# A gather-and-sum graph layer on one core: parts of x taken from its bytes, and the counts dealt to the turns from a table

## The chip, the cores and the metric

The kernel runs on one core of one Trainium2 chip. The metric is the time of one execution on the device, in microseconds. Three runs of the kernel before are given, and one further execution was profiled; all times of single instructions come from that one.

## The reference

One layer of a graph network with two kinds of edges, then a residual sum and a layer norm. There are 12500 nodes of 128 features, and 400000 edges, sorted by `dst`.

```python
Xs = X[src]
m_data = Xs @ W_data.T + b_data
m_ctrl = Xs @ W_control.T + b_control
msg = jnp.where((edge_types == 0)[:, None], m_data, m_ctrl)
agg = jax.ops.segment_sum(msg, dst, num_segments=X.shape[0])
out = jax.nn.relu(agg + (X @ W_self.T + b_self))
x = _layernorm(X + out, axis=-1)          # over the features, eps 1e-5, no scale, no shift
```

## The kernel before

**What it sums.** The weights are applied after the sums. For every node and each kind of edge the kernel sums the rows `x[src]` of its edges, and counts the edges (for the biases). Since the edges are sorted by `dst`, a stretch of edges touches few nodes, and a sum is a matrix product of rows with a 0/1 selection: rows on the partitions, two kinds times 88 nodes (176 columns) as the moving side.

**Exact rows from bf16.** A float32 row would be slow in the matrix engine, so x is split into three bf16 parts that add up to it, 384 columns instead of 128. They lie in SBUF (`x3`, 98 blocks of 128 nodes) and in DRAM (`rows3`). In `split_x` x is fetched in 8 pieces (six of 14 blocks, one of 13, and the last, partial block), four ahead of use, by DMAs on ScalarE's queue. Of each piece (`split`) ScalarE copies x to bf16 (the high part, line 262), VectorE subtracts that from x (line 263), ScalarE copies the rest to bf16 (the middle part, line 264), and VectorE subtracts again (the low part, line 265). The pieces are then stored to `rows3` on SP's queue.

**Two ways to the rows.** The 3125 chunks of 128 edges fall into 25 groups of 125 chunks, each with five runs of 5 chunks ("p") and five of 20 ("e"); in 18 of the groups the last e run is taken as p instead. A p chunk fetches its 128 rows from `rows3` by an indirect DMA on GpSimd's queue (line 754, tile `msg`). The 107 e windows `w` need no such fetch: their 2560 edges are sorted by the source's block of 128 nodes into 100 cells of 32 places (`block_matrix` to `keep_codes`: products on VectorE, small matrix products, a round trip through DRAM with the tiles `there` and `pick`), and the rows are picked out of `x3` by matrix products with a 0/1 matrix of 128 nodes by 32 places (line 820, `got<-x,pick`). Four blocks share a product's 128 output partitions, each in its own quarter of 32 columns of the array. Edges that find their cell full are fetched by an indirect DMA as well (line 798, tile `last`, one for each window).

**A window's turns.** In `picked`, the 25 fours of blocks of a window go in five turns, bounds 0, 5, 10, 15, 19, 24. Turn `t` picks the rows of its fours into PSUM (`rows`), ScalarE copies them to bf16 (line 834, tile `emsg`), VectorE makes selections (`choose`, line 504: 10 fours in turn 0, 9 in turn 1, 6 in turn 3, from two buffers), and TensorE adds the rows of the turn before to the window's sums (`add`, line 704, full width). The turn of 3 also picks the last, half four (quarters 2 and 3). Before `add`, `count` (line 842) adds up the edges of each four: a product of 32 columns, `one_col`, with the selection, put into quarter `q % 4`:

```python
cells_of(s["ps"], EW, 1)[CAP * (q % 4):CAP * (q % 4 + 1), :], one_col[:, :CAP], s["sel"][q],
```

The turns 1 to 4 count 5, 5, 5 and 4 fours; the end of the window, which is run within turn 0 of the next one, counts 6. The quarters are added up when a group is finished, so it does not matter which of them a four is counted in. `accumulate` then adds the window's sums to the group's (line 743).

**Order.** Units of work are merged by a position within the window (`merged`, `evenly`), and a scheduler of the framework sets the order of instructions on each engine from there; `issue_after` holds work behind a given instruction. `paced` lets a gather start behind a given matrix product.

**The opening.** Before the first window the kernel makes its tables, splits x (one unit a piece, `split_units`), prepares the e edges of group 0 (`prep_e`), sorts windows 0 and 1 (`all_slots`), computes where each window's sums go (`places_and_weights`), and stores `rows3`. Then the loop over the windows starts. A second, slow path for inputs on which the sorting overflows (`long_path`) is skipped at the end by a branch.

## Time and profile before

| what | us |
|---|---|
| median of 3 runs | 1758.43 |
| lowest and highest run | 1756.07, 1759.98 |
| the profiled execution | 1757.87 |
| its span, first to last instruction | 1756.1 |
| TensorE busy (matrix products) | 1615.3 |
| VectorE busy | 1595.2 |
| GpSimd busy | 1316.6 |
| ScalarE busy | 1229.2 |

PE is TensorE, PEld its weight loads, DVE VectorE, ACT ScalarE, POOL GpSimd, and SP the engine that issues most DMAs. A row of a group gives line, engine, operation, output and inputs with their shapes, the count, then the busy time and the mean of one in ns, then the idle time ahead of these instructions and who ended it. A row of the timeline gives the start, the duration, the engine and the same names, with the idle time in brackets; neighbouring instructions of one line are merged, and the duration runs to the end of the last. Matrix products overlap in the pipeline, so the distance from one start to the next tells more than a duration. A name with a q behind the engine is its queue: it waits or issues.

### The profile page before, as it was taken

What the parts mean: (1) busy time and instruction counts of PE and PEld (TensorE: products, weight loads), DVE (VectorE), ACT (ScalarE), POOL (GpSimd) and SP (SyncE); (2) the same over time, 40 slices, a digit from 0 to 9 for tenths busy, and PEclk for the clock granted to TensorE, in tenths of its full rate; (3) what the DMA queues carried; (4) which work ended last, traced back from release to release, by engine and by line L of the source; (5) the groups of instructions that cost most, each with busy time, mean ns of one, the idle gap of its engine ahead of it and who ended that gap; (6) DMA issues with size and microseconds to landing.
All of it is one profiled execution on the core that took longest, in us unless ns stands there. A gap on an engine that the chain in (4) does not pass through costs nothing.

```text
span 1756.1 us, 72083 instructions
## 1 busy us (share of the span) xinstructions
PE 1615.3 (92%) x29945; PEld 1311.7 (75%) x29945; DVE 1595.2 (91%) x3996; ACT 1229.2 (70%) x2249; POOL 1316.6 (75%) x1109
## 2 busy tenths in 40 slices
PE   0599999999999999999999999999999989999997
PEld 0377777777778777777877877777777777878786
DVE  8899999998999998999988999999999989999993
ACT  4577777767677667767766777776777766767675
POOL 0288877787777787877887877887877877777871
PEclk9999999999999999999999999999999999999999
DMA  8655454446454545444535454544454535544441
GB/s 237 209 165 160 128 158 136 147 125 199 115 164 134 159 125 179 143 152 127 166 119 164 150 164 133 164 122 147 160 159 135 158 108 162 167 139 141 151 139 41
DMA packets 190562, 261.28 MB, mean 149 GB/s; under 512 B 86437, under 2 KB 155983, under 8 KB 187152
## 3 DMA queue, kind: packets, MB, share of 16 engines
q1 hardware_dynamic: 126894, 148.02, 25.9%
q0 software_dynamic: 50704, 102.16, 20.8%
q10 hardware_dynamic: 12626, 6.40, 1.2%
q8 instruction: 236, 3.87, 0.9%
q14 instruction: 102, 0.84, 0.1%
HBM read 238.47 MB, written 18.00 MB: 146 GB/s over the span
## 4 chain that ended last, share of the span: by engine, by line
PE 48%; DVE 32%; issue 6%; DMA 6%; ACT 5%; DVEq 1%; POOL 1%; SPq 0%; POOLq 0%; ACTq 0%
PE sums L704 22%; PE got L820 15%; DVE esel L504 3%; PE side L950 3%; DVE pick L690 3%; PE sums L842 3%; DMA last<-rows,idx 3%; DVE rv L635 2%; ACT emsg L834 2%; DVE prod L598 2%; DVE prod L576 2%; PE side L584 2%; DVE acc L743 2%; PE side L647 2%; DVE ahead L594 2%
## 5 line engine op out<-in xcount | busy, mean ns | idle before, releaser
L754 POOL DMA_INDIRECT msg<-rows,pidx x985 | 1190.9, 1209 | 307.5 <-issue 118.9
L834 ACT CAST emsg<-got 128x768 bf16<-128x768 f32 (+1 forms) x1070 | 951.9, 930 | 303.9 <-PE got L820 289.8
L704 PE MATMUL sums<-esel,emsg 128*128 128x176 bf16 x7704 | 683.4, 240 | 0.0
L704 PEld LDWEIGHTS <-emsg 128*128 128x128 bf16 x7704 | 566.9, 98 | 68.7 <-issue 28.5
L820 PE MATMUL got<-x,pick 128*32 128x384 bf16 x10486 | 568.0, 330 | 21.9 <-DVE pick L690 14.7
L820 PEld LDWEIGHTS <-pick 128*32 128x32 bf16 x10486 | 239.2, 96 | 139.2 <-issue 20.6
L504 DVE TENSOR_TENSOR esel<-code_col,code 128x1760 bf16<-128x1760 bf16 x321 | 292.7, 912 | 13.6 <-PE sums L704 11.6
L798 POOL DMA_INDIRECT last<-rows,idx x107 | 122.0, 1141 | 106.0 <-DVE pick L690 63.7
L704 PE MATMUL sums<-psel,msg 128*128 128x48 bf16 x2955 | 184.2, 184 | 17.2 <-DVE acc L743 15.2
L842 PE MATMUL sums<-esel,one_col 128*32 128x176 bf16 x2675 | 193.7, 240 | 4.4 <-DVE acc L743 4.4
L704 PEld LDWEIGHTS <-msg 128*128 128x128 bf16 x2955 | 149.9, 97 | 36.2 <-issue 31.4
L842 PEld LDWEIGHTS <-one_col 128*32 128x32 bf16 x2675 | 111.9, 97 | 60.7 <-issue 4.1
L790 PE MATMUL sums<-psel,one_col 128*128 128x48 bf16 x985 | 150.2, 183 | 0.0
L743 DVE TENSOR_TENSOR acc<-acc,sums 128x352 f32 (+2 forms) x232 | 99.4, 430 | 40.4 <-PE sums L704 36.8
L504 DVE TENSOR_TENSOR O<-cell_col,blk 128x2000 bf16<-128x2000 bf16 x107 | 128.2, 1198 | 2.1 <-issue 2.1
L598 DVE TENSOR_TENSOR prod<-O,ahead 128x2000 bf16<-128x2000 bf16 x107 | 127.6, 1193 | 0.1
L690 DVE TENSOR_SCALAR pick<-pick,lane_f 128x3200 bf16<-128x3200 bf16 x107 | 113.2, 1058 | 0.0
L647 PE MATMUL side<-rv,O 128*128 128x64 bf16 x2140 | 83.3, 195 | 31.6 <-DVE rv L635 30.6
L647 PEld LDWEIGHTS <-O 128*128 128x128 bf16 x2140 | 78.7, 100 | 33.3 <-DVE rv L635 29.3
L594 DVE TENSOR_REDUCE ahead<-side 128x100 bf16<-128x500 f32 x107 | 72.2, 675 | 28.0 <-PE side L520 27.3
L790 PEld LDWEIGHTS <-one_col 128*128 128x128 bf16 x985 | 94.3, 96 | 0.0
L635 DVE TENSOR_TENSOR rv<-rm,vals 128x1280 bf16<-128x1280 bf16 x107 | 87.8, 821 | 0.3
(170 smaller groups left out, 1869.2 us busy)
## 6 DMA issues: line engine op xcount, KB each, us to landing
pick<-there SPq DMA_DIRECT2D x107, 800.0 KB
acc<-acc_start SPq DMA_DIRECT2D x23, 1280.0 KB
msg<-rows,pidx POOLq DMA_INDIRECT x985
rows<-x SPq DMA_DIRECT2D x6, 1344.0 KB
xs<-in_x_dram SPq DMA_DIRECT2D x99, 62.5 KB
out_dram<-h SPq DMA_DIRECT2D x99, 62.5 KB
xt<-in_x_dram ACTq DMA_DIRECT2D x6, 896.0 KB
there<-cell SPq DMA_DIRECT2D x107, 6.2 KB
```

Of the source, the lines that this page charges most:

```text
L504: nc.vector.tensor_tensor(sel.rearrange("p n (w t) -> p n w t", t=2), col[:rows].rearrange("p (o w t) -> p o w t", o=1, t=2).to_broadcast( ...
L598: nc.vector.tensor_tensor(prod, s["O"], ahead.rearrange("p (o j) -> p o j", o=1).to_broadcast([P, EC, NCELL]), op=OP.mult)
L635: placed[:] = [nc.vector.tensor_tensor(rv.rearrange("p c v (r t) -> p c v r t", t=2), rm.rearrange("p c (o r t) -> p c o r t", o=1, t=2).t ...
L647: nc.tensor.matmul(s["rk"][:m, :2 * CAP], s["held"][:, c * NCELL:c * NCELL + m], s["rv"][:, c].rearrange("p v r -> p (v r)"), start=(c == ...
L690: nc.vector.tensor_scalar(t, t, lane_f, None, op0=OP.is_equal)
L704: last = nc.tensor.matmul(out, msg[:, j * D:(j + 1) * D], sel, start=(start and j == 0), stop=stop, skip_group_check=True)
L743: added.append(nc.vector.tensor_add(win, win, ps[:, :4 * wide].rearrange("p (a w) -> p a w", w=wide)[:, :, :width]))
L754: return nc.gpsimd.indirect_dma_start(out=msg, out_offset=None, in_=rows3[:, :], in_offset=bass.IndirectOffsetOnAxis(ap=codes["p", g][0][: ...
L790: nc.tensor.matmul(cnt, one_col, sel, start=False, stop=(c == n - 1), skip_group_check=True)
L820: last = nc.tensor.matmul(ps[CAP * a:CAP * (a + 1), :], slots[w]["pick"][:, a * NQ + q, :], x3[:, 4 * q + a - a0].rearrange("p j d -> p (j ...
L834: nc.scalar.copy(msg[:, :n], ps[:, :n, :3 * D])
L842: nc.tensor.matmul(cells_of(s["ps"], EW, 1)[CAP * (q % 4):CAP * (q % 4 + 1), :], one_col[:, :CAP], s["sel"][q], start=(q < 4), stop=(q + 4 ...
```

## The change

The two parts below the high one are now made from the bytes of the float itself. ScalarE copies the upper 16 bits of each float to the high part; it also copies the second and the first byte, as numbers scaled by 2^-15 and 2^-23, to the middle and the low part. VectorE takes sign and exponent of the high part by an AND on 16-bit integers (tile `power`, a power of two) and multiplies both lower parts by it, in place.

The counts are dealt from a table, `quarters`: 4, 4, 8 and 3 fours in the turns 1 to 4, and 6 at the end, each with the quarter of the array written out.

Beside that the opening is put in another order. The e preparation of group 0 comes ahead of the pieces of x and behind the tables, the pieces behind the last instruction of that preparation; small pieces of `places_and_weights` come earlier; window 0's round trip through DRAM goes over GpSimd's queue instead of SP's; loads and the p preparation of group 0, and later each e preparation, are held behind the latest `rv` product (`placed[0]`).

```diff
@@ -258,11 +260,19 @@
 
         def split(b, m, rows):
             t = tiles.pop(b)
-            h, mm, lo = (x3[:rows, b:b + m, j, :] for j in range(3))
-            nc.scalar.copy(h, t)
-            nc.vector.tensor_sub(t, t, h)
-            nc.scalar.copy(mm, t)
-            parted.append(nc.vector.tensor_sub(lo, t, mm))
+            part = x3[:rows, b:b + m]
+            byte = t.bitcast(U8).rearrange("p k (d b) -> p k d b", b=4)
+            nc.scalar.copy(part[:, :, 0, :], t.bitcast(BF).rearrange("p k (d b) -> p k d b", b=2)[:, :, :, 1])
+            for j in range(2):
+                nc.scalar.activation(part[:, :, 2 - j, :], byte[:, :, :, j], AF.Copy, scale=2.0 ** (8 * j - 23))
+            power = pool.tile([P, step, D], BF, name="power", bufs=2)[:rows, :m, :]
+            nc.vector.tensor_single_scalar(
+                power.bitcast(I16), part[:, :, 0, :].bitcast(I16), -128, op=OP.bitwise_and
+            )
+            parted.append(nc.vector.tensor_tensor(
+                part[:, :, 1:, :], part[:, :, 1:, :],
+                power.rearrange("p k (j d) -> p k j d", j=1).to_broadcast([rows, m, 2, D]), op=OP.mult,
+            ))
 
         def store():
             for b, m, rows in pieces:
@@ -275,7 +285,8 @@
             fetch(*p)
         for k, p in enumerate(pieces):
             def unit(k=k, p=p):
-                split(*p)
+                with tc.issue_after(ready.ins):
+                    split(*p)
                 if k + ahead < len(pieces):
                     fetch(*pieces[k + ahead])
             units.append(unit)
@@ -342,7 +353,7 @@
         nc.vector.tensor_single_scalar(t, t, P - 1, op=OP.bitwise_and)
     nc.vector.tensor_copy(own_f, own)
     for a in range(4):
-        nc.vector.tensor_scalar(ltri[:, a, :], free[:, a, :], own_f[:, a:a + 1], None, op0=OP.is_gt)
+        tables = nc.vector.tensor_scalar(ltri[:, a, :], free[:, a, :], own_f[:, a:a + 1], None, op0=OP.is_gt)
     one_col = keep.tile([P, P], BF, name="one_col")
     nc.vector.memset(one_col, 0.0)
     nc.vector.memset(one_col[:, 0:6], 1.0)
@@ -354,11 +365,27 @@
     nc.vector.memset(worst, 0.0)
     over_n = keep.tile([P, len(each_e)], BF, name="over_n")
 
+    from_i = tmp.tile([rows_p, 1], I32, name="from_i")
+    from_f = tmp.tile([rows_p, 1], FP, name="from_f")
+    nc.gpsimd.iota(from_i, pattern=[[0, 1]], base=-PAD, channel_multiplier=DPC)
+    nc.vector.tensor_copy(from_f, from_i)
+    steps = {}
+    for k in range(1, NE):
+        steps[k] = tmp.tile([rows_p, 1], FP, name=f"ge{k}")
+        nc.vector.tensor_scalar(
+            steps[k], from_f, float(DPC * PB * k - PAD), float(-DPC * PB), op0=OP.is_ge, op1=OP.mult
+        )
+    for k in range(1, NE):
+        nc.vector.tensor_add(from_f, from_f, steps[k])
+    least = tmp.tile([1, NG, NWIN], FP, name="least")
+    for i, (_, _, c, _) in enumerate(windows(0)):
+        nc.vector.memset(least[:, :, i:i + 1], float(max(0, c * DPC - PAD)))
     halves = tmp.tile([1, 2, NG * NE], I32, name="halves")
     nc.vector.memset(x3[:, NBLK - 1], 0.0)
     first = first_i["e"].rearrange("o g w -> o (g w)")
-    nc.vector.tensor_single_scalar(halves[:, 0, :], first, 7, op=OP.logical_shift_right)
-    nc.vector.tensor_single_scalar(halves[:, 1, :], first, 127, op=OP.bitwise_and)
+    with tc.issue_after(tables.ins):
+        nc.vector.tensor_single_scalar(halves[:, 0, :], first, 7, op=OP.logical_shift_right)
+        nc.vector.tensor_single_scalar(halves[:, 1, :], first, 127, op=OP.bitwise_and)
     halves_b = tmp.tile([1, 2, NG * NE], BF, name="halves_b")
     nc.vector.tensor_copy(halves_b, halves)
     fin0 = side()
@@ -373,25 +400,11 @@
 
     def places_and_weights():
         near = raw["near"] = keep.tile([rows_p, NG], FP, name="near")
-        from_i = tmp.tile([rows_p, 1], I32, name="from_i")
-        from_f = tmp.tile([rows_p, 1], FP, name="from_f")
-        nc.gpsimd.iota(from_i, pattern=[[0, 1]], base=-PAD, channel_multiplier=DPC)
-        nc.vector.tensor_copy(from_f, from_i)
-        for k in range(1, NE):
-            ge = raw[f"ge{k}"] = tmp.tile([rows_p, 1], FP, name=f"ge{k}")
-            nc.vector.tensor_scalar(
-                ge, from_f, float(DPC * PB * k - PAD), float(-DPC * PB), op0=OP.is_ge, op1=OP.mult
-            )
-        for k in range(1, NE):
-            nc.vector.tensor_add(from_f, from_f, raw.pop(f"ge{k}"))
         nc.vector.tensor_scalar(near, near_i, from_f, None, op0=OP.add)
         place = tmp.tile([1, 2, NG, NWIN], FP, name="place")
         ref = tmp.tile([1, NG, NE, 2], I32, name="ref")
         nc.gpsimd.iota(ref, pattern=[[GN, NG], [0, NE], [-PAD, 2]], base=PAD - M0, channel_multiplier=0)
         ref = ref.rearrange("o g e k -> o g (e k)")
-        least = tmp.tile([1, NG, NWIN], FP, name="least")
-        for i, (_, _, c, _) in enumerate(windows(0)):
-            nc.vector.memset(least[:, :, i:i + 1], float(max(0, c * DPC - PAD)))
         for at, k in enumerate("pe"):
                 each = place[:, 0].rearrange("o g (i k) -> o g i k", k=2)[:, :, :, at]
                 nc.vector.tensor_tensor(
@@ -491,8 +504,9 @@
         nc.vector.scalar_tensor_tensor(pk, s, 256.0, code, op0=OP.mult, op1=OP.add)
         vals2 = pre.tile([P, n, 2, 2], BF, name="vals2", bufs=3)
         for v, val in enumerate((parts[:, 1, :], code)):
-            nc.scalar.copy(vals2[:, :, v, :], val.rearrange("p (n o) -> p n o", o=1).to_broadcast([P, n, 2]))
+            last = nc.scalar.copy(vals2[:, :, v, :], val.rearrange("p (n o) -> p n o", o=1).to_broadcast([P, n, 2]))
         codes["e", g] = (blk, twice("blk2", parts[:, 0, :]), vals2, pk)
+        return last
 
 
     slots, placed = {}, []
@@ -654,9 +668,10 @@
             cell = s["cell"] = two.tile([P, 2 * CAP], BF, name="cell")
             nc.scalar.copy(cell, s["rk"][:, :2 * CAP])
             there = scr.tile([NCELL, CAP], BF, name="there")
-            nc.sync.dma_start(out=there[:, :], in_=cell[:NCELL, :CAP])
+            queue = nc.sync if w else nc.gpsimd
+            queue.dma_start(out=there[:, :], in_=cell[:NCELL, :CAP])
             pick = s["pick"] = two.tile([P, NCELL, CAP], BF, name="pick")
-            nc.sync.dma_start(
+            queue.dma_start(
                 out=pick.rearrange("p j r -> p (j r)"),
                 in_=there.rearrange("(o j) r -> o (j r)", o=1).to_broadcast([P, NCELL * CAP]),
             )
@@ -836,13 +851,21 @@
                 nc.scalar.copy(s["msg"][NQ - 1][OVF:, :], ps[OVF:, n, :3 * D])
             return last
 
-        def count(q):
-            if q == 0:
-                s["ps"] = sums()
-            nc.tensor.matmul(
-                cells_of(s["ps"], EW, 1)[CAP * (q % 4):CAP * (q % 4 + 1), :], one_col[:, :CAP], s["sel"][q],
-                start=(q < 4), stop=(q + 4 >= NQ), skip_group_check=True,
-            )
+        quarters = {1: "0123", 2: "0123", 3: "01010123", 4: "012", 5: "301230"}
+        assert sum(map(len, quarters.values())) == NQ
+        cells = [(t, int(a)) for t, row in quarters.items() for a in row]
+
+        def count(t):
+            for q, (at, a) in enumerate(cells):
+                if at != t:
+                    continue
+                if q == 0:
+                    s["ps"] = sums()
+                same = [k for k, (_, b) in enumerate(cells) if b == a]
+                nc.tensor.matmul(
+                    cells_of(s["ps"], EW, 1)[CAP * a:CAP * (a + 1), :], one_col[:, :CAP], s["sel"][q],
+                    start=(q == same[0]), stop=(q == same[-1]), skip_group_check=True,
+                )
 
         def add(q0, q1):
             done = [
@@ -868,8 +891,7 @@
             if t == 3:
                 choose(19, NQ - 19)
             if t > 0:
-                for q in range(bounds[t - 1], bounds[t]):
-                    count(q)
+                count(t)
             if t == 1 and before:
                 before()
             if t > 0:
@@ -882,8 +904,7 @@
 
         def end():
 
-            for q in range(bounds[turns - 1], NQ):
-                count(q)
+            count(turns)
             early, *more = tiled.get(turns, [lambda: None])
             early()
             gates = add(bounds[turns - 1], NQ)
@@ -1026,8 +1047,9 @@
         units = begin_slots(w) + [u for _, u in begun.pop(w)]
         return units + [u for t in sorted(slots[w]["tiled"]) for u in slots[w]["tiled"][t]]
 
+    with tc.issue_after(tables.ins):
+        ready = prep_e(0)
     split_units.pop(0)()
-    prep_e(0)
     merged([(1.5, lambda: places_after(parted[2]))], evenly(all_slots(0) + all_slots(1)), evenly(split_units))
     bparts()
     early.close()
@@ -1041,10 +1063,11 @@
     store_rows()
     spare_rows(0)
     bias_rows()
-    load(1, "e")
-    load(1, "p")
-    for u in prep_p(0):
-        u()
+    with tc.issue_after(placed[0].ins):
+        load(1, "e")
+        load(1, "p")
+        for u in prep_p(0):
+            u()
 
 
     chunks, closed, rest = {}, {}, []
@@ -1063,11 +1086,15 @@
     def ending():
         pass
 
+    def later(g):
+        with tc.issue_after(placed[0].ins):
+            prep_e(g)
+
     for w in range(pairs):
         g, i = each_e[w]
         more = []
         if i == 1 and g + 1 < NG:
-            more.append((0.1, lambda: prep_e(g + 1)))
+            more.append((0.1, lambda: later(g + 1)))
         if i == 1 and g + 1 < NG:
             more += evenly(prep_p(g + 1), 0.1, 0.7)
         if i == 3 and g + 2 < NG:
```

2 lines of the change are left out of this document (added).

## The prediction

> **What bounds the kernel now.** I read the page first (engine shares, the chain that ended last, the groups), then the timeline of the opening and of two steady windows, then the busy table of stretches, then the waits.
>
> ```profile
> span 1756.1 us, 72083 instructions
> PE 1615.3 (92%) x29945; PEld 1311.7 (75%) x29945; DVE 1595.2 (91%) x3996; ACT 1229.2 (70%) x2249; POOL 1316.6 (75%) x1109
> PE 48%; DVE 32%; issue 6%; DMA 6%; ACT 5%; DVEq 1%; POOL 1%; SPq 0%; POOLq 0%; ACTq 0%
> L842 PE MATMUL sums<-esel,one_col 128*32 128x176 bf16 x2675 | 193.7, 240 | 4.4 <-DVE acc L743 4.4
> ```
>
> TensorE is busy 92% of the span and stands for 48% of the chain, VectorE 91% and 32%: two engines take turns as the bound. The busy table tells where:
>
> ```profile
> 25.00:50.00 25.00, 1.28 (x20) 1.15 (x20) 22.34 (x30) 11.39 (x7) 0.00 (x0) 1.00 1.09 340
> 50.00:68.00 18.00, 3.46 (x45) 2.67 (x45) 15.47 (x55) 5.58 (x14) 0.00 (x0) 1.00 0.86 272
> 805.10:818.60 13.50, 13.50 (x278) 11.19 (x276) 12.75 (x29) 9.92 (x19) 10.41 (x10) 1.00 0.43 133
> 1023.20:1043.40 20.20, 19.34 (x318) 15.55 (x320) 18.41 (x51) 12.17 (x28) 15.94 (x15) 1.00 0.46 148
> ```
>
> (Columns: stretch, length, then busy us of PE, weight loads, VectorE, ScalarE, GpSimd; clock, DMA share, GB/s.) Until 68 us TensorE hardly works: that is the opening, in which x is split and the first windows are prepared; VectorE is its busiest engine, ScalarE has room. Afterwards a quiet window (third row) is TensorE's alone, 13.50 of 13.50 us, VectorE 12.75. A window that also finishes a group (fourth row) leaves TensorE 0.86 us idle and VectorE 1.79: neither bounds it throughout.
>
> **Part 1, the counts.** A turn has picks (32 columns wide), counts (32 wide), then full-width sums:
>
> ```profile
> 808.88 0.32 PE L842 MATMUL sums<-esel,one_col 128*32 128x176 bf16 x5
> 809.13 0.41 PE L584 MATMUL side<-prod,ltri 128*128 128x125 bf16 x4
> 811.66 0.32 PE L842 MATMUL sums<-esel,one_col 128*32 128x176 bf16 x5
> 811.91 1.31 PE L704 MATMUL sums<-esel,emsg 128*128 128x176 bf16 x15
> 814.01 0.24 PE L842 MATMUL sums<-esel,one_col 128*32 128x176 bf16 x2
> 814.01 0.33 PE L820 MATMUL got<-x,pick 128*32 128x384 bf16 x2
> 814.17 0.32 PE L842 MATMUL sums<-esel,one_col 128*32 128x176 bf16 x3
> 814.42 1.31 PE L704 MATMUL sums<-esel,emsg 128*128 128x176 bf16 x15
> 816.68 0.25 PE L842 MATMUL sums<-esel,one_col 128*32 128x176 bf16 x4
> 816.87 0.33 PE L704 MATMUL sums<-esel,emsg 128*128 128x176 bf16 x2
> ```
>
> First column start, second duration. Four counts, one to each quarter of the columns, hold the next full-width product back by 816.87 - 816.68 = 0.19 us; five cost 811.91 - 811.66 = 0.25 (and 809.13 - 808.88 = 0.25), because the fifth needs a quarter that is taken. So a second wave costs 0.06 us. The third counted turn (814.01) shows quarters working side by side: two counts start with the two half picks, three follow at 814.17, again two waves: 0.41 us in all.
>
> The table deals 4, 4, 8, 3, 6. Turns 1 and 2: one wave each, -0.06 us each. Turn 3 has "01010123": the half picks hold quarters 2 and 3 until 814.17, 0.16 us, in which quarters 0 and 1 take two counts each (0.06 to 0.08 apart); the last four are one wave, so 0.16 + 0.19 = 0.35 instead of 0.41, -0.06, though three counts more are done there. Turn 4 with three instead of four: still one wave, 0. The last turn keeps its six in the same quarters, 0. Sum 0.18 to 0.2, say 0.19 us a window, 107 windows: 20 us if each were on the path, 0 if none. The page gives the share: 48 / 92 = 52% of TensorE's busy time lies on the chain, hence **-10.5 us**.
>
> Some of it is given back. GpSimd fetches all gathered rows:
>
> ```profile
> L754 POOL DMA_INDIRECT msg<-rows,pidx x985 | 1190.9, 1209 | 307.5 <-issue 118.9
> L798 POOL DMA_INDIRECT last<-rows,idx x107 | 122.0, 1141 | 106.0 <-DVE pick L690 63.7
> PE sums L704 <- DMA last<-rows,idx: 15.2, 11, 4.5
> ```
>
> Each gather is followed by a gap of 307.5 / 985 = 0.31 us, so the quiet window above is full for GpSimd too: 10.41 + 10 x 0.31 = 13.5 of 13.50 us. The long window makes 15 gathers in 20.20 us, more than the mean of 1092 / 107 = 10.2, so there GpSimd catches up what it owes. The spare rows (`last`) stand in the same queue, and TensorE has waited for them 11 times (third row, 15.2 us). With some four quiet windows before each such wait shortened by 0.19, each may grow by 0.76 us, 8 us at most and 0 at least; I take a quarter, **+2 us**.
>
> What this adds: the counts of blocks 8 and 9 move from turn 2 to turn 3, and they read the first selection tile, whose buffer the third selection (1056 wide) takes over. VectorE's third selection must now wait for them.
>
> ```profile
> 813.84 0.70 DVE L504 TENSOR_TENSOR esel<-code_col,code 128x1056 bf16<-128x1056 bf16 x1
> 817.14 1.04 DVE L690 TENSOR_SCALAR pick<-pick,lane_f 128x3200 bf16<-128x3200 bf16 x1
> 818.58 0.51 PE L820 MATMUL got<-x,pick 128*32 128x384 bf16 x8
> ```
>
> In a quiet window it runs at 813.84, before the counts (814.01 + 0.24 = 814.25). Left there it would stall VectorE 0.41 us, with rank, rv and the next pick queued behind it, and the pick ends (817.14 + 1.04 = 818.18) only 0.4 us before the next window's first picks at 818.58. But the instruction order of the changed kernel puts it behind the pick in 53 of the 107 windows, the quiet ones nearly all, where it is needed only by the six counts about 1 us into the next window; in the other windows VectorE is mostly late and finds the counts done. I cost it at 0 and make the other case a rival. The preparation of the next group's e edges, now held behind the rv product of the window before, keeps its work: 0.
>
> **Part 2, the opening.** All terms from the first 68 us, by shape:
>
> ```profile
> L263 DVE TENSOR_TENSOR xt<-xt,x 128x1792 f32<-128x1792 f32 x6 | 12.1, 2014 | 0.0
> L265 DVE TENSOR_TENSOR x<-xt,x 128x1792 bf16<-128x1792 f32 x6 | 12.1, 2014 | 2.5 <-ACT x L264 2.5
> L264 ACT CAST x<-xt 128x1792 bf16<-128x1792 f32 x6 | 10.1, 1684 | 8.4 <-DVE xt L263 8.4
> L262 ACT CAST x<-xt 128x1792 bf16<-128x1792 f32 x6 | 10.0, 1681 | 0.0
> L598 DVE TENSOR_TENSOR prod<-O,ahead 128x2000 bf16<-128x2000 bf16 x2 | 2.4, 1190 | 0.0
> L690 DVE TENSOR_SCALAR pick<-pick,lane_f 128x3200 bf16<-128x3200 bf16 x1 | 1.0, 1030 | 0.0
> 12.56 0.41 DVE L342 TENSOR_SCALAR i<-i 128x512 int32<-128x512 int32 x1
> ```
>
> Six full pieces and one of 13 blocks make 7 in round numbers (the last block is 0.3 us an instruction). VectorE loses 2 x 2.01 = 4.03 us a piece. It gains a product of 3584 bf16 elements: by L598, 1.19 x 3584 / 2000 = 2.1. And an AND of 1792 int16: by L690 (16 bit, one tensor) 1.03 x 1792 / 3200 = 0.6; by L342 (the same operation on int32) 0.41 x 3.5 = 1.4. I take 0.6, its width being that of L690. So 2.7 instead of 4.03, -9 us over seven pieces (-4 with 1.4). [...] No run here shows an int16 AND yet.
>
> ScalarE gets three passes instead of two: 3 x 1.69 = 5.05 a piece, +1.69, +12 us in seven. A read of single bytes, four apart, has no row; I take the f32 row, and bound it by twice that (+23 us more in 14 passes) and, below, by nothing gained. ScalarE then needs no answer from VectorE within a piece (the 8.4 us of waits of L264 go), and an xt buffer is free as soon as ScalarE has read it.
>
> ```profile
> 14.29 0.35 ACT L450 CAST blk<-parts 128x200 bf16<-128x200 int32 x1
> 24.32 0.42 SPq L291 DMA_DIRECT2D brow<-in_L_gnn_b_self_dram  x1
> 23.75 1.40 ACTq L257 DMA_DIRECT2D xt<-in_x_dram  x2
> 46.85 1.58 ACT L262 CAST x<-xt 128x1664 bf16<-128x1664 f32 x1 [7.52 <-DMA rows<-x]
> 66.91 1.03 DVE L690 TENSOR_SCALAR pick<-pick,lane_f 128x3200 bf16<-128x3200 bf16 x1
> 68.00 2.57 PE L820 MATMUL got<-x,pick 128*32 128x384 bf16 x28 [1.94 <-DVE pick L690]
> 71.26 1.95 DVE L504 TENSOR_TENSOR esel<-code_col,code 128x1760 bf16<-128x1760 bf16 x2
> 72.94 0.67 PE L842 MATMUL sums<-esel,one_col 128*32 128x176 bf16 x5
> ```
>
> Today ScalarE stands 7.52 us in its own queue: the fetch of the last x block waits until an earlier store of rows has landed. In the new order that fetch waits only for small loads and the fetch before it, and the stall goes. Running the new order through: ScalarE ends the e copies of group 0 at about 13.3 us (before, 14.29 + 0.35, but now ahead of x), then seven pieces at 5.05: 48.7 us if nothing stops it. Three things do. The fetch of piece 4 still waits for a small load on SP's queue (23.75 in the old run), 3.5 us. The copy of the spare bits of window 0 stands in front of piece 3 and waits for VectorE, which itself waits about 3.5 us for brow (issued at 24.32, now read early by the bias parts): 3 us. The cell copies and the last fetch: some 2 us. So ScalarE ends at 57 to 58. VectorE's pick for window 0 stands behind the product of piece 5, about 54; TensorE's first picks start near 55 instead of 68.00, their eviction waits for ScalarE at 58, and the first selection, queued behind the product of piece 6 (58), the small last block and the p preparation (1.5 us), runs at 61.5 instead of 71.26. The stores of rows end near 63 to 64 (the DMA engines moved 340 GB/s from 25 to 50 us, and at 25 us there remain 9.6 MB of rows, 12500 x 768 bytes, and 2.7 MB of x, the pieces after the fourth: 36 us), and the spare gather needs them only at the end of window 0. Sum: **-9.5 us**, range -12 to -4 from the AND and the stalls, worse only if byte reads are dear. The copies of window 0's cells over GpSimd's queue are issued near 40, 14 us ahead of their reader: 0. If that cover went, GpSimd's next work, the spare gather, would start later, not TensorE.
>
> **The sum.** The profiled execution took 1757.87 us (span 1756.1 and 1.8 around it), 0.56 below the median. 1757.87 - 10.5 + 2 - 9.5 = 1739.9; with 0.56, 1740.4, so 1740 us.
>
> **Rivals.**
> GpSimd becomes the bound of the loop. Gathers and their gaps fill 1190.9 + 307.5 + 122.0 + 106.0 - 63.7 = 1663 of the 1688 us after 68. If these spans are work and not waiting, a faster TensorE only waits longer for the spare rows, and the loop returns nothing: 1758.4 - 9.5 = 1749. For it speaks the full quiet window, against it that GpSimd catches up in the long ones and that TensorE has waited for rows 15.2 us in all. Chance 0.2.
>
> The opening does not pay (bytes read dearer, or the stalls add up), the counts do: 1758.4 - 8.5 = 1750. Chance 0.1.
>
> Slower: the third selection stalls VectorE ahead of the counts in the 54 windows where it still stands before the pick, 0.41 us each, 22 us, and VectorE cannot make it up. With nothing from the counts and the opening intact: 1758.4 - 9.5 + 22 = 1771; with 10.5 us from the counts, 1760. It decides where VectorE comes there more than 0.2 us ahead of the counts; in the old times that is the case in few of these windows. Byte reads at twice the price (+23 us in the opening, of which about 10 hide where ScalarE would have waited) would end at the same place. Chance 0.1 together.
>
> That the quarters are not taken as dealt (turn 3 in program order, one wave more) costs 0.06 x 107 x 0.52 = 3.5 us, 1744: part of the forecast's range.
>
> **How the numbers follow.** Forecast 0.6, GpSimd 0.2, opening 0.1, slower 0.1. The forecast's own range is 1730 (20 us of counts) to 1746 (4 us from the opening); for 8 in 10 it reaches to the two partial cases: 1730 to 1752. A measurement here can tell about 0.2%, 3.5 us. Faster 0.86, same 0.05, slower 0.09.
>
> **What would show it.** Counts of four followed after 0.19 us by sums in turns 1 and 2, and eight within 0.35 in turn 3; quiet windows of about 13.3 us; x passes of 1.69 on ScalarE, products of 2.1 and ANDs of 0.6 on VectorE; the first pick near 55, the first selection near 61.5. Wrong if byte passes take over 2 us, if quiet windows stay at 13.5, or if the waits for the spare rows grow by 10 us.

## The result: 28 us slower, and the profile after

| | before | changed |
|---|---|---|
| median of 6 runs, us | 1755.78 (1752.09 to 1759.98) | 1783.88 (1778.16 to 1786.98) |
| ratio to before | 1 | 1.0151, 95% interval 1.0132 to 1.0170 |
| profiled execution, span, us | 1756.1 | 1783.3 |

The forecast was 1740 us, with a range of 1730 to 1752. First the page of the changed kernel: engines, then the share of each in the chain that ended last; then two rows of the groups by shape (busy us, mean ns, idle time before and what ended it).

```profile
span 1783.3 us, 72078 instructions
PE 1613.3 (90%) x29945; PEld 1302.2 (73%) x29945; DVE 1595.6 (89%) x3996; ACT 1237.8 (69%) x2257; POOL 1339.8 (75%) x1111
PE 43%; DVE 35%; issue 6%; ACT 6%; DMA 6%; DVEq 1%; POOL 1%; SPq 0%; ACTq 0%; POOLq 0%
L865 PE MATMUL sums<-esel,one_col 128*32 128x176 bf16 x2675 | 172.2, 241 | 1.2 <-DVE acc L758 1.1
L682 PE MATMUL side<-ident_b,cell 128*32 128x25 bf16 x428 | 26.5, 182 | 14.2 <-ACT cell L669 13.7
```

The counts do what the table promised: 172.2 us of TensorE instead of 193.7, 21.5 / 107 = 0.20 us a window. But TensorE's total fell by 2.0 us only (1615.3 to 1613.3), so its other work takes some 19.5 us more; and it is idle for 1783.3 - 1613.3 = 170.0 us, where it was idle for 140.8. The waits (total us, times, longest) of TensorE, GpSimd and ScalarE, and last ScalarE's in the kernel before:

```profile
PE sums L719 <- DMA last<-rows,idx: 41.3, 16, 7.6
POOL msg L769 <- PE got L835: 74.0, 234, 1.3
ACT bits_b L643 <- DVE bits L641: 70.0, 66, 5.1
ACT bits_b L629 <- DVE bits L627: 47.6, 56, 3.6
```

The waits for the spare rows grew from 15.2 to 41.3 us: that alone is 26 of the 29 us of idle time. ScalarE also waits 22 us longer for VectorE's bits, which follow the pick. Rows of the timeline, VectorE and GpSimd before and after, then TensorE, show how one such wait comes about:

```profile
357.88 3.51 POOL L754 DMA_INDIRECT msg<-rows,pidx  x1 [0.30 <-PE sums L704]
359.53 1.04 DVE L690 TENSOR_SCALAR pick<-pick,lane_f 128x3200 bf16<-128x3200 bf16 x1
360.50 0.17 DVE L615 MAX8 top<-key 128x8 f32<-128x20 f32 x1
361.76 4.10 POOL L769 DMA_INDIRECT msg<-rows,pidx  x1 [0.30 <-issue]
363.38 1.04 DVE L705 TENSOR_SCALAR pick<-pick,lane_f 128x3200 bf16<-128x3200 bf16 x1
364.35 0.69 DVE L518 TENSOR_TENSOR esel<-code_col,code 128x1056 bf16<-128x1056 bf16 x1
364.96 0.17 DVE L629 MAX8 top<-key 128x8 f32<-128x20 f32 x1
368.21 2.70 POOL L813 DMA_INDIRECT last<-rows,idx  x1 [0.30 <-issue]
373.17 0.62 PE L719 MATMUL sums<-esel,last 128*128 128x176 bf16 x3 [5.35 <-DMA last<-rows,idx]
```

The first three rows are the kernel before. The gather here started within VectorE's rv and lasts through its unbroken stretch rv, prod, eq, prod, pick: 3.51 us, where the shortest gathers take 0.91 to 0.94. In the changed kernel the third selection, 0.69 us, stands behind the pick, and the gather takes 4.10. The gather of the spare rows, which stands behind it in GpSimd's queue, starts at 368.21; TensorE has been ready since 367.8 and stands still for 5.35 us. Then this, in the table of stretches (columns as in the prediction):

```profile
363.00:367.80 4.80, 4.80 (x100) 3.75 (x90) 4.80 (x17) 2.97 (x6) 4.50 (x2) 1.00 0.13 33
367.80:373.17 5.37, 0.02 (x2) 0.01 (x1) 2.32 (x3) 1.92 (x2) 4.45 (x4) 0.83 0.63 199
373.17:376.50 3.33, 3.33 (x46) 2.17 (x47) 1.41 (x2) 1.83 (x6) 2.42 (x4) 0.50 0.25 71
376.50:380.00 3.50, 3.50 (x54) 3.01 (x53) 3.18 (x5) 1.40 (x3) 2.70 (x3) 0.77 0.31 84
```

After the stall the granted clock is 0.50 for the whole 3.3 us of the third row and 0.77 on average in the fourth: this wait is paid for twice. Twenty picks take 1.57 us there to the start of the next product (374.23 to 375.80), and 0.82 at 1.00 (378.73 to 379.55). Over the execution the mean clock is 0.984 (0.995 before). Apart from the idle end of the span, the stretches at 0.50 hold 37.2 us of TensorE's busy time, 10.2 before. By the two times of the picks, I estimate that the 27 us more would have taken about half as long at 1.00: some 13.5 of the 19.5 us of extra TensorE time are the clock's; where the other 6 come from stays open.

The opening, its passes by shape and then its landmarks:

```profile
L265 ACT COPY x<-xt 128x1792 bf16<-128x1792 bf16 x6 | 10.1, 1677 | 0.3 <-ACT bits_b L643 0.3
L267 ACT ACTIVATE x<-xt 128x1792 bf16<-128x1792 uint8 x12 | 19.7, 1688 | 4.2 <-DMA ptyp<-in_edge_type_dram 3.6 <-DMA xt<-in_x_dram 0.5
L269 DVE TENSOR_SCALAR power<-x 128x1792 int16<-128x1792 int16 x6 | 3.7, 614 | 0.0
L272 DVE TENSOR_TENSOR x<-x,power 128x3584 bf16<-128x3584 bf16 x6 | 12.1, 2017 | 2.0 <-ACT code L692 2.0
59.60 1.46 PE L835 MATMUL got<-x,pick 128*32 128x384 bf16 x13 [2.62 <-DVE pick L705]
62.25 0.38 SPq L279 DMA_DIRECT2D rows<-x  x1
64.28 1.95 DVE L518 TENSOR_TENSOR esel<-code_col,code 128x1760 bf16<-128x1760 bf16 x2
72.35 0.96 POOL L813 DMA_INDIRECT last<-rows,idx  x1 [24.03 <-ACT emsg L849]
68.07 2.96 POOL L798 DMA_INDIRECT last<-rows,idx  x1 [63.74 <-DVE pick L690]
```

TensorE's first picks come 8.4 us earlier (59.60, was 68.00). GpSimd's first gather comes 4.3 us later: 72.35, and in the kernel before (last row) 68.07. It needs the stored rows; the last large store is issued at 62.25 only, and the DMA engines fall quiet near 71 (their busy share is 0.25 from 70 to 71 us, 0.01 from 71 to 72). From its first gather to its last GpSimd is idle, beyond the 0.305 us that lie between two gathers in the median (0.303 at least), for some 17 us of 1685 (before, some 17 of 1663).

### The profile page after: what moved, and what is told of

Read it like the earlier page. It is cut to its first block, busy times and chain, and to the rows that moved or that the text cites. A ratio compares the mean times of both kernels' runs of the same rounds, so it can differ in the third digit from the quotient of the medians.

```text
span 1783.3 us, 72078 instructions
## 1 busy us (share of the span) xinstructions
PE 1613.3 (90%) x29945; PEld 1302.2 (73%) x29945; DVE 1595.6 (89%) x3996; ACT 1237.8 (69%) x2257; POOL 1339.8 (75%) x1111
## 3 DMA queue, kind: packets, MB, share of 16 engines
q8 instruction: 236, 3.87, 0.9%
## 4 chain that ended last, share of the span: by engine, by line
PE 43%; DVE 35%; issue 6%; ACT 6%; DMA 6%; DVEq 1%; POOL 1%; SPq 0%; ACTq 0%; POOLq 0%
PE sums L719 19%; PE got L835 14%; DVE esel L518 4%; ACT emsg L849 3%; DVE pick L705 3%; DMA last<-rows,idx 3%; PE side L971 3%; DVE prod L612 3%; DVE rv L649 2%; DMA msg<-rows,pidx 2%; DVE prod L590 2%; DVE ahead L608 2%; DVE found L621 2%; DVE acc L758 2%; PE sums L865 2%
## 5 line engine op out<-in xcount | busy, mean ns | idle before, releaser
L769 POOL DMA_INDIRECT msg<-rows,pidx x985 | 1208.2, 1227 | 305.4 <-issue 139.0
L835 PE MATMUL got<-x,pick 128*32 128x384 bf16 x10486 | 574.0, 332 | 27.4 <-DVE pick L705 17.6
L813 POOL DMA_INDIRECT last<-rows,idx x107 | 126.5, 1182 | 68.8 <-ACT emsg L849 27.1
L865 PE MATMUL sums<-esel,one_col 128*32 128x176 bf16 x2675 | 172.2, 241 | 1.2 <-DVE acc L758 1.1
L865 PEld LDWEIGHTS <-one_col 128*32 128x32 bf16 x2675 | 91.7, 97 | 42.3 <-issue 4.5
L608 DVE TENSOR_REDUCE ahead<-side 128x100 bf16<-128x500 f32 x107 | 72.3, 675 | 37.2 <-PE side L534 36.9
```

The lines of the kernel that those rows point to most:

```text
L769: return nc.gpsimd.indirect_dma_start(out=msg, out_offset=None, in_=rows3[:, :], in_offset=bass.IndirectOffsetOnAxis(ap=codes["p", g][0][: ...
L813: return nc.gpsimd.indirect_dma_start(out=msg[:OVF, :], out_offset=None, in_=rows3[:, :], in_offset=bass.IndirectOffsetOnAxis(ap=slots[w][ ...
L835: last = nc.tensor.matmul(ps[CAP * a:CAP * (a + 1), :], slots[w]["pick"][:, a * NQ + q, :], x3[:, 4 * q + a - a0].rearrange("p j d -> p (j ...
L865: nc.tensor.matmul(cells_of(s["ps"], EW, 1)[CAP * a:CAP * (a + 1), :], one_col[:, :CAP], s["sel"][q], start=(q == same[0]), stop=(q == sam ...
```

## The experiments

**Theory and rivals.** GpSimd sets the end (G); the table harms because it moves the third selection behind the pick (S), and the selection there lengthens the gathers (H). Rivals: the opening leaves the loop in a bad phase (O), the held preparation does it (P), VectorE's order does it whatever GpSimd does (V).

The runs come in sets; each set has a chip of its own and runs of the kernel before beside it. Between sets, ratios compare better than times.

**One part at a time.** The table alone, put into the kernel before:

```diff
-        def count(q):
...
+        quarters = {1: "0123", 2: "0123", 3: "01010123", 4: "012", 5: "301230"}
...
+        def count(t):
...
```

> The kernel before with the table of counts alone (4, 4, 8, 3, 6); opening as before. Theory S (selection): the table moves the third selection behind the pick in about half of the windows, where it lengthens VectorE's unbroken stretch by 0.70 us; this costs the loop some 36 us, so this kernel takes 1785 to 1792 us, its order has the third selection behind the pick in 59 of 106 windows, and the waits for the spare rows are 35 to 60 us as in the changed kernel (40.7), not 15.2. Rival O (the opening leaves the loop in a bad phase: GpSimd starts late and the spare rows stay late): the table alone does no harm, 1740 to 1752 us.

1774.68 us beside 1755.37; ratio 1.0110 (1.0086 to 1.0134). S is right in sign, but sized too high. The waits for the spare rows are 23.5 us, below the 35 to 60 that S asked for (41.3 in the whole change).

The opening alone, with the hold: the changed kernel with the old `count(q)`.

> The changed kernel with the old dealing of counts (5, 5, 5, 4, 6, four to a wave); the opening by bytes, the held preparation and all orders of the opening stay. Theory S: the third selection stands ahead of the pick again in 105 of 106 windows and the opening's gain shows: 1746 to 1752 us. Rival O: 1775 us or more, with the 7.6 us stall in the third window still there.

1758.91, ratio 1.0027 (1.0007 to 1.0046). Neither was right: no harm to speak of, and no gain either. The first gather is at 73.35 us; one stall of 8.8 us follows:

```profile
73.35 0.97 POOL L813 DMA_INDIRECT last<-rows,idx  x1 [24.81 <-ACT acc L740]
PE sums L719 <- DMA last<-rows,idx: 15.6, 3, 8.8
```

The changed kernel with fours 8 and 9 counted in turn 2 again:

```diff
-        quarters = {1: "0123", 2: "0123", 3: "01010123", 4: "012", 5: "301230"}
+        quarters = {1: "0123", 2: "012301", 3: "010123", 4: "012", 5: "301230"}
```

> The changed kernel with the table 4, 6, 6, 3, 6: fours 8 and 9 are counted in turn 2 again (two waves there), the rest as dealt. Theory S: the third selection stands ahead of the pick in 105 of 106 windows; 0.12 us a window are saved, 107 x 0.12 x 0.52 = 6.7 us, so 1739 to 1748 us. Rival O: 1770 us or more. If instead the dealing of the counts over the quarters itself were slow, also 1770 us or more, but with short waits for the spare rows.

1769.16, ratio 1.0071 (1.0043 to 1.0100), and its nine runs fall into two heaps, 1759 to 1762 and 1769 to 1778. S, which expected 1739 to 1748, does not explain that: the selection is ahead of the pick in 105 windows. The profiled execution is of the upper heap and waits 37.6 us for spare rows. I read it so that, where GpSimd has no slack, little decides whether a stall happens; no run shows it.

The changed kernel without the hold on the next group's e edges:

```diff
     def later(g):
-        with tc.issue_after(placed[0].ins):
-            prep_e(g)
+        prep_e(g)
```

> The changed kernel without the hold on the preparation of the next group's e edges (it is issued where the scheduler puts it, as before). Theory S: the third selection stays behind the pick in 59 of 106 windows, so the loss stays: 1778 to 1790 us. Rival P (the held preparation pushes VectorE's chain to the bits in each group's second window, and ScalarE's cell copy stands behind it): the loss of some 1 us in 20 to 25 windows and what follows from it goes, 1755 us or less.

1774.67, ratio 1.0117 (1.0090 to 1.0143): as much as the table alone, and 9.2 us less than the whole change by the medians, 6 by the ratios (1.0151), whose intervals overlap. Both expectations missed. So the hold costs some 6 to 9 us beside the table, not sharply measured. TensorE's wait for the cell copy points at it, as idle time of the products that read it:

```profile
L682 PE MATMUL side<-ident_b,cell 128*32 128x25 bf16 x428 | 27.0, 183 | 8.1 <-ACT cell L669 7.5 <-issue 0.2
```

8.1 us, as against 14.2 in the whole change and 6.9 in the kernel before.

**GpSimd's load.** Every fifth gather left out; its chunk is summed from the rows of the chunk before, so the sums are not the reference's:

```diff
         fetched.append(msg)
+        if to_fetch and len(to_fetch) % 5 == 0:
+            to_fetch.pop(0)
+            fetched.append(msg)
```

> The kernel before with every fifth gather of GpSimd left out (its chunk is summed from the rows of the chunk before, so the gathered sums are not the reference's): 985 gathers become about 788, all other work stays. Theory G (GpSimd bounds the loop: from its first gather to its last it works back to back): 197 gathers of about 1.5 us with their gaps are gone, the loop runs at TensorE's and VectorE's pace, 1700 to 1735 us, and the waits for the spare rows (15.2 us) fall under 5. Rival V (TensorE and VectorE bound it, GpSimd's long gathers are slack): 1750 to 1758 us.

> The changed kernel with every fifth gather left out in the same way. Theory G: with GpSimd out of the way the change gains what the prediction summed for TensorE and the opening, so 8 to 20 us under the kernel before with fewer gathers. Rival V (the third selection behind the pick delays VectorE's chain to the bits, the cell copy and the next window, whatever GpSimd does): 15 to 28 us above it. Rival C (the stalls lower TensorE's clock): as G here, since the stalls go with the waits.

> The kernel before with the table 4, 4, 8, 3, 6 and with every fifth gather left out as in the two runs with fewer gathers (its chunk is summed from the rows of the chunk before). Theory G (the table's loss is GpSimd's): the loss of 19 us against the same kernel with the old counts goes, 1732 to 1744 us beside 1740.6. Rival V (the loss is VectorE's order): 1750 to 1760 us. If the counts' 10.5 us were on the path once GpSimd is out of it: 1728 to 1733 us.

| every fifth gather left out | us | ratio to before |
|---|---|---|
| kernel before | 1740.63 (1736.92 to 1741.49) | 0.9921 (0.9893 to 0.9948) |
| the table alone | 1735.73 (1733.93 to 1737.04) | 0.9880 (0.9853 to 0.9906) |
| the whole change | 1743.86 (1740.29 to 1750.56) | 0.9949 (0.9929 to 0.9969) |

This is the experiment that tells most. With GpSimd full, the table costs 19 us; with GpSimd relieved it costs nothing: 4.9 us less by the medians, 7 by the ratios. (The table was run in another set than the other two rows, and the intervals just overlap, so the gain itself is not certain.) The whole change costs 28 us, and 3.2 with GpSimd relieved. V, which expected the table's loss to stay, is out. A fifth of the gathered bytes goes with the gathers; no run separates that from GpSimd's own time. The engines and GpSimd's waits of the relieved kernel before, the same waits in the kernel before, and the engines of the relieved table:

```profile
PE 1608.2 (93%) x29945; PEld 1308.6 (75%) x29945; DVE 1592.8 (92%) x3996; ACT 1227.4 (71%) x2249; POOL 1104.8 (64%) x913
POOL msg L757 <- PE got L823: 166.1, 241, 4.0
POOL msg L754 <- PE got L820: 80.5, 249, 3.6
PE 1593.0 (92%) x29945; PEld 1294.4 (75%) x29945; DVE 1596.8 (92%) x3996; ACT 1228.7 (71%) x2249; POOL 1118.1 (64%) x913
```

In the kernel before these waits are little more than the gap of 0.3 us each; relieved, they are twice as long, and in all GpSimd is idle 268 us beyond the gaps instead of 17. It is in time, so it has to wait. TensorE no longer waits for spare rows at all. G asked for more than it got, though (1700 to 1735): some 14 us below, by their shares, VectorE and TensorE are the next bound.

G also missed for the whole change: it was to gain 8 to 20 us on the relieved kernel before, and lost 3.2; it is 8 us slower than the relieved table. Two waits of TensorE in it, and the second in the relieved table:

```profile
PE sums L719 <- DMA last<-rows,idx: 7.6, 1, 7.6
PE side L682 <- ACT cell L669: 14.1, 17, 5.7
PE side L667 <- ACT cell L655: 8.8, 7, 6.8
```

The one stall of 7.6 us, in the third window, takes what the opening gained: the first picks come 8.4 us earlier than in the relieved kernel before (59.37, was 67.72), the eleventh window begins 1 us later. The waits for cells, which the hold lengthens, are as long as with GpSimd full. So what the table loses hangs on GpSimd's load in the loop; what the opening and the hold lose does not, as far as these runs tell.

**The hold.** An extra instruction of 0.51 us behind the pick in 52 windows of the kernel before, once a selection, once a reduction, in the same instruction order:

```diff
+                if w % 2 and w > 2:
+                    extra = big.tile([P, 4, 2 * EW], BF, name="extra")
+                    select(extra, code_col, slots[w]["code"][:, :4])
```

> The kernel before with an extra selection on VectorE (128 x 704, two SBUF inputs, about 0.5 us) right behind the pick in 52 of the 107 windows; its result is not used. Theory H (VectorE's unbroken stretch rv, prod, eq, prod, pick keeps a GpSimd gather from ending, so whatever is queued behind the pick lengthens that gather, and GpSimd bounds the loop): gathers over 4 us in 8 to 15 windows instead of 1, GpSimd's busy time 10 to 26 us up, the time 10 to 30 us up: 1766 to 1786 us. Rival V (only VectorE's own time counts): 52 x 0.5 = 26 us more work at 91% busy, so some 8 to 24 us up, but then the reduction of equal length costs the same.

> As the run with the extra selection, but the extra instruction is a reduction of one SBUF tensor (128 x 352 to 2 columns, about 0.5 us) at the same places in the same order. Theory H: a reduction holds GpSimd off less or not at all, so no more long gathers than before, GpSimd's busy time up by less than 8 us and the time by 0 to 8 us: 1755 to 1764 us. Rival V: as the extra selection, within 4 us.

1775.69, ratio 1.0114 (1.0086 to 1.0143), and 1766.13, ratio 1.0075 (1.0047 to 1.0104): 21.4 us for the selection and 11.8 for the reduction, with VectorE busy for 1614.1 us in both. So about half is VectorE's time and half depends on the kind of instruction, though the two intervals still overlap. V (within 4 us) missed, and H too: its own sign, gathers over 4 us in 8 to 15 windows, did not appear (5, and 2). GpSimd's busy time is 1326.1 and 1319.4. One and the same window, first with the selection, then with the reduction, shows what the kind does:

```profile
370.25 3.95 POOL L757 DMA_INDIRECT msg<-rows,pidx  x1 [0.30 <-PE sums L707]
371.90 1.04 DVE L690 TENSOR_SCALAR pick<-pick,lane_f 128x3200 bf16<-128x3200 bf16 x1
364.13 3.51 POOL L759 DMA_INDIRECT msg<-rows,pidx  x1 [0.30 <-PE sums L709]
365.78 1.04 DVE L690 TENSOR_SCALAR pick<-pick,lane_f 128x3200 bf16<-128x3200 bf16 x1
```

With the reduction behind the pick the gather ends 0.82 us behind the pick (367.64, 366.82), as in the kernel before; with the selection 1.26 us behind it. Four more pairs of windows with a gather that started in rv show the same (1.23 to 1.51 us, against 0.82). But that is five gathers with 0.4 to 0.7 us each: the direct hold is shown, and it is small beside the 9.6 us between the two runs.

The third selection behind the bits, with the table (4, 4, 8, 3, 6) in the kernel before:

```diff
-            if t == 3:
-                choose(19, NQ - 19)
+            if t == 4:
+                with tc.issue_after(coded[0].ins):
+                    choose(19, NQ - 19)
```

> The kernel before with the table 4, 4, 8, 3, 6, and the third selection issued behind the last of the bits in every window, so that it neither lengthens the stretch rv to pick that a gather sits through nor stands ahead of the bits. Theory S with the hold on GpSimd as its price: gathers over 4 us back to 1 to 3 (8 with the table alone), 1745 to 1760 us. Rival B (what costs is that the selection is late for the next window's work, wherever it stands behind the pick): 1772 us or more, as with the table alone (1774.7).

1791.99, ratio 1.0197 (1.0169 to 1.0224). S with the hold as its price missed, and B, that the selection is late for the next window wherever it stands behind the pick, came true. Gathers over 4 us fell to 1 (8 with the table alone), but those over 1.5 us rose from 168 to 218, GpSimd's busy time to 1359.0 and the waits for spare rows to 39.0 us. The selection is out of the stretch to the pick, but in one with the first selection and O, and later for its own readers; which of the two costs the time was not separated.

```profile
PE 1611.8 (90%) x29945; PEld 1305.4 (73%) x29945; DVE 1604.6 (90%) x3996; ACT 1235.7 (69%) x2249; POOL 1359.0 (76%) x1109
```

**Less change.** The table 4, 6, 6, 3, 6 in the kernel before, and the opening with the old counts and without the hold:

> The kernel before with the table 4, 6, 6, 3, 6 and nothing else: 0.12 us of counts saved a window, the third selection ahead of the pick in 104 of 106 windows. Theory S (the table costs time only where it moves the third selection): no loss, 1748 to 1757 us. Rival L (GpSimd has no slack, so any work taken off TensorE only makes it arrive earlier at rows that are not there, stall, and run at half clock afterwards): 1760 to 1770 us, with waits for the spare rows of 25 us or more instead of 15.2.

> The changed opening with the old counts and without the hold on the preparation of the next group's e edges. Theory R (the opening returns what it gains, because GpSimd's first gather waits for the stores of the x parts and comes 5 us later, 73.4 us instead of 68.1, and GpSimd works back to back from there): 1752 to 1760 us, the first pick near 60 and one stall of 6 to 10 us on the spare rows within the first six windows. Rival P (the hold alone spoils the opening's gain): 1744 to 1750 us.

1760.03, ratio 1.0019 (0.9999 to 1.0039), and 1759.46, ratio 1.0011 (0.9992 to 1.0030). 0.12 us a window taken from TensorE, or 8 us from its start, change nothing that can be told. For the smaller table that lies between S and L, and the waits for spare rows (17.0 us) are not the 25 of L; for the opening the time is what R expected, with two stalls of 5.0 and 7.0 us in the first windows.

**A split of the stretch, and a later start.** In the split, prod, eq and prod stand behind the bits instead of ahead of the pick; in the other kernel six extra gathers stand ahead of GpSimd's first. The edit of the split:

```diff
...
-            return tc.issue_after(placed[0].ins) if w > 1 else ExitStack()
+            return tc.issue_after(coded[0].ins) if w > 2 else ExitStack()
...
-            more += [(0.55, lambda: [u() for u in begin_slots(w + 3)])]
+            more += [(0.78, lambda: [u() for u in begin_slots(w + 3)])]
```

> The kernel before with prod, eq, prod of the window after next issued behind the last of the bits instead of between rv and the pick: the stretch rv, prod, eq, prod, pick (3.3 us) becomes rv, pick (1.85 us), and a new stretch prod, eq, prod, selection, O (3.6 us) stands behind the bits. All work stays. Theory H (unbroken stretches of VectorE hold GpSimd's gathers, GpSimd sets the end): the time goes with GpSimd's busy time, whichever way: 1 us of span for each us of it, within 6 us. If only the stretch rv to pick counted, 1735 to 1750 us; if the new stretch holds gathers just as long, 1750 to 1775. Rival V (VectorE's order to the pick and bits): the pick and the bits come 1.4 us earlier in each window, so 1735 to 1750 us whatever GpSimd's busy time does.

> The same split with the table 4, 4, 8, 3, 6. Theory H: the third selection now stands behind a pick that has only rv ahead of it, so its 0.70 us makes a stretch of 2.55 us and not 4.0; the table costs 0 to 8 us against the split alone instead of 19. Rival B (the late selection itself costs): 15 to 20 us more than the split alone.

> The kernel before with six extra gathers (the first spare rows again, into tiles that nothing reads) ahead of GpSimd's first one; they take some 1.25 us each with their gaps, of which 2.2 us lie in its wait for the first indices, so the gathers of the loop begin 4 to 6 us later. Theory R (a later start of GpSimd goes through to the end, which is why the changed opening, with its first gather at 73.4 instead of 68.1 us, gains nothing): 1758 to 1764 us, 3 to 7 us up. Rival (the first windows have rows in hand, fetched 14 ahead, and hide it): no change, 1753 to 1757 us.

> The split alone again (prod, eq, prod of the window after next behind the bits, old counts, old opening), on another chip. Theory H: the time follows GpSimd's busy time, 1 us of span for each us, within 6 us; in the split's run on the other chip gathers over 3.3 us fell from 13 to 2 and those over 1.5 us rose from 154 to 213, so 1740 to 1760 us. Rival V (VectorE's order alone, pick and bits 1.4 us earlier): 1735 to 1750 us whatever GpSimd's busy time does.

> The split with the table 4, 4, 8, 3, 6, old opening. Theory H: 0 to 8 us more than the split alone, or less than it, since the third selection lengthens a stretch of 1.85 us only. Rival B (the late selection itself costs): 15 to 20 us more than the split alone.

> The changed opening, the table 4, 4, 8, 3, 6 and the split together, without the hold on the preparation of the next group's e edges. Theory R (the opening's gain is returned because GpSimd's first gather comes 5 us later): within 5 us of the split with the table. If the split gives GpSimd the slack to make up those 5 us: 5 to 8 us less than it.

In these two sets of runs the kernel before itself took 2104.86 and 2074.13 us, so only the ratios within a set count:

| kernel | first set, ratio | second set, ratio |
|---|---|---|
| split | 0.9933 (0.9910 to 0.9956) | 0.9936 (0.9911 to 0.9961) |
| split and table | 0.9944 (0.9919 to 0.9969) | 0.9953 (0.9929 to 0.9977) |
| split, table and opening, no hold | | 0.9934 (0.9912 to 0.9956) |
| six gathers ahead | 1.0041 (1.0018 to 1.0063) | |

```profile
PE 1770.8 (85%) x29945; PEld 1376.9 (66%) x29945; DVE 1611.4 (77%) x3996; ACT 1240.3 (59%) x2249; POOL 1318.9 (63%) x1109
```

This is the split in the first set: TensorE's share is the largest, VectorE and GpSimd have room. GpSimd is not full here, and so these runs cannot tell H from V, nor show that a later first gather goes through to the end where it is full. What they do show: the split is 0.65% faster than the kernel before, twice; and with room on GpSimd the table costs 0.3 us in the first set and 4.7 in the second, both within the intervals, not the 15 to 20 of B. It does not gain either, though it takes 22 and 19 us off TensorE's busy time there. The opening without the hold gains 3.6 us beside the table, also within the intervals. Six gathers ahead cost 7 us even here, as R had it (3 to 7), without one wait for spare rows. Whether the split also beats the kernel before at 1755 us wasn't measured.

**GpSimd's busy time and the time.** The kernels with all 1092 gathers, of the sets in which the kernel before took 1754 to 1757 us:

| kernel | GpSimd busy | median |
|---|---|---|
| opening alone | 1305.5 | 1758.91 |
| table 4, 6, 6, 3, 6 alone | 1315.3 | 1760.03 |
| before | 1316.6 | 1755.78 |
| extra reduction | 1319.4 | 1766.13 |
| opening, no hold | 1320.0 | 1759.46 |
| opening, 4, 6, 6, 3, 6 | 1322.3 | 1769.16 |
| extra selection | 1326.1 | 1775.69 |
| change without hold | 1327.0 | 1774.67 |
| table alone | 1330.1 | 1774.68 |
| change | 1339.8 | 1783.88 |
| late third selection | 1359.0 | 1791.99 |

The medians follow it, 0.75 us for each, within 8 us (correlation 0.93); the busy time is that of the one profiled execution. This table alone doesn't say which of the two is the cause; the runs with fewer gathers do.

## Why the prediction was wrong, by its own steps

- **Waves of counts, -0.06 in three turns.** Right: 0.20 us a window by the counts' own rows; in the relieved pair TensorE's busy time falls by 15.2 us with the table, 0.14 a window. The sign named for it, quiet windows of 13.3 us, hardly showed: the median of the windows under 14 us went from 13.56 to 13.50. **-10.5 us from it:** wrong. The price was TensorE's share of the chain that ended last, 52%. A chain names who came last at each step, not who has room: with GpSimd relieved the table was worth some 5 us, and with GpSimd full less than nothing. The chain by line was a lower price at hand: the page of the kernel before gives the counts (`PE sums L842`) 3% of the span, some 53 of their 194 us.
- **+2 us given back by the spare rows.** This term of the sum failed: the waits grew by 26 us, and brought the half clock with them. The argument was that GpSimd catches up in the long windows; 17 us of idle time in 1663 say that it never does. That these waits grow by 10 us was one of the prediction's own signs of being wrong.
- **Third selection at 0.** This step failed. The instruction order was read rightly (behind the pick in 54 of 106 windows here); the reading stopped at who needs the selection. What it stands in front of (the bits) and what runs beside it (GpSimd's gathers) was not priced. Of GpSimd's 21.7 us more in gathers, the gathers that run beside a pick have 29.7 (144 of them, 233.9 us; before, 137, 204.2), the others 8 less. Those that started before rv was done and met the pick take 4.07 us on average (15 of them) instead of 3.14 (14). In seven of these the third selection follows the pick, and all seven end 1.44 us behind the pick, where 0.82 is usual: 0.62 us each, some 4 us in all, is what the selection adds by standing there. In the table alone there are only 9 such gathers, of 3.87 us, and yet GpSimd's gathers take 13.4 us more in all. So the direct hold is the smaller part. How much of the 19 us comes by longer gathers and how much by later bits and cells stays open: the extra selection against the extra reduction says half and half, with the limits given there.
- **Held preparation at 0.** Wrong by some 6 to 9 us beside the table (1783.88 against 1774.67); the idle time in front of the products on the cells went from 8.1 to 14.2 us. With the old counts it costs nothing that can be told (1758.91 against 1759.46, in different sets).
- **Opening, -9.5 us.** The prices were right: 1.68 and 1.69 us a pass on ScalarE, 2.02 for the product, 0.61 for the AND (0.6 predicted, after the pick's 1.03 us for 3200 elements). The first picks came at 59.6 (55 predicted), the first selection at 64.3 (61.5). The step that failed is the end of the stores, 63 to 64 us in the prediction and near 71 in the trace, and with it the sentence that a later start of GpSimd would cost TensorE nothing. It costs all of the gain: in the third window TensorE waits 7.6 us for spare rows, with GpSimd relieved in the loop as well.

```profile
92.15 5.20 POOL L769 DMA_INDIRECT msg<-rows,pidx  x1 [0.30 <-issue]
97.65 0.91 POOL L813 DMA_INDIRECT last<-rows,idx  x1 [0.30 <-issue]
102.90 0.62 PE L719 MATMUL sums<-esel,last 128*128 128x176 bf16 x3 [7.64 <-DMA last<-rows,idx]
```

- **The sum.** By these runs: table +19.3, opening without the hold 0 (the change without the hold, 1774.67, less the table alone, 1774.68), hold +9.2: 28.5 us, and 28.1 were measured. Each of the last two terms is the difference to the run before it, so that the sum must come out: it is a reading of the shares, not a proof.
- **The rivals.** GpSimd as the bound of the loop had 0.2 and named the right engine; its price, "the loop returns nothing", was too kind, because it left out that the table itself makes GpSimd's work longer. The slower rival looked for the third selection ahead of the counts; it was the windows in which it stands behind.

## What to carry to other kernels

An engine can be full at 75% busy, as GpSimd is here with 0.305 us between its short instructions: add the gaps before you call it free, and ask of each moved instruction what it lengthens on the full engine, not only who waits for its result. Where three engines are all nearly full, a share of the chain is no price for work saved; take load off the suspect and see whether the edit pays then. A gain at the start of one engine may be none if another, which it soon waits for, starts later.

## What the runs showed that was not expected

- **TensorE at half clock after a stall.** After 5.37 us without work the granted clock was 0.50 for 3.3 us and 0.77 in the 3.5 us behind (rows above). All clock records of the two traces, before and changed, are 1.00 or 0.50, so the four rows place the half clock from 371.3, 3.5 us into the stall, to 378.1, 4.9 us after it. In the changed kernel, behind the opening, each of TensorE's six waits of 3.4 us and more (3.41 to 7.64) has such a stretch; it begins 2.5 to 4.3 us after the wait began and lasts 3.4 to 10.2 us. Shorter waits differ: in the kernel before, 1.41 us without work was followed by 3.41 us at 0.50 (rows below), and 3.04 us without work, at 897.05, by 1.00 throughout the next 4.9 us. What decides it, these traces do not show. The two rows of the 1.41 us:

```profile
446.22:447.63 1.41, 0.00 (x1) 0.00 (x1) 1.41 (x5) 0.97 (x3) 1.41 (x1) 1.00 0.04 12
448.22:451.63 3.41, 3.41 (x42) 2.61 (x39) 2.77 (x9) 2.03 (x3) 2.80 (x3) 0.50 0.73 256
```

- **A gather ends just behind the pick.** In the profiled execution of before 73 gathers start no later than a pick (to 0.02 us) and end behind it; 58 of them end 0.10 to 0.13 us behind its end. One pair from the changed kernel, ends 399.97 and 400.10:

```profile
398.93 1.04 DVE L705 TENSOR_SCALAR pick<-pick,lane_f 128x3200 bf16<-128x3200 bf16 x1
398.93 1.17 POOL L769 DMA_INDIRECT msg<-rows,pidx  x1 [0.30 <-issue]
```

Which part of a gather is held up, no row shows. What stands behind the pick tells: the extra selection (a tensor_tensor) put the gather's end off from 0.82 to 1.26 us, the reduction, 0.51 us as against 0.52, did not (rows above). It matters when the gather starts: in the kernel before, of the 41 that started behind rv and over 0.5 us ahead of the pick, 34 took at most 1.33 us.

- **The same kernel at 2105 us.** In two sets of runs the kernel before took 2104.86 and 2074.13 us instead of 1755. VectorE's pick took 1.05 us in the split there, 1.06 in the kernel before here; TensorE's busy time was 1770.8 us in the split instead of some 1615, and it stood 153.5 us in waits that the profile puts down to no instruction ("issue"), of which the kernel before at 1756 us has none. Why wasn't found.
